# Bilinear interaction of 496 feature pairs: all of w in the first line of loads, one part turned in its own buffer, and the last batch tile stored in six groups, one of them by GpSimd's queue

## The chip, the cores and the metric

The kernel runs on one core of a Trainium2 chip. A core has five engines: TensorE (PE, matrix products), VectorE (DVE), ScalarE (ACT), GpSimd (POOL) and SyncE (SP, which here only issues transfers). Data moves between HBM and the on-chip memory SBUF through 16 DMA engines, which all queues share. The metric is the device time of one execution in microseconds (us), lower is better.

## The reference

There are 4096 samples with 32 feature vectors of 64 floats each, and for every pair of features (i, j) with i < j, 496 pairs in all, a 64 x 64 matrix. Each output vector is feature i times the pair's matrix, multiplied element by element with feature j. All is float32. The output has 4096 x 496 x 64 x 4 bytes = 520 MB; x has 33.6 MB, w 8.1 MB.

```python
B, F, D = (4096, 32, 64)
idx_i, idx_j = np.triu_indices(F, k=1)
vi = inputs[:, idx_i, :]
vj = inputs[:, idx_j, :]
vidots = jnp.einsum('bpd,pde->bpe', vi, W)
return vidots * vj
```

## The kernel before

The batch is cut into 16 blocks of 256 samples, each of two batch tiles of 128 samples (one to a partition). The 496 pairs are cut into five groups of 90, 97, 99, 105 and 105 pairs. The products of one tile and group gather in one of three buffers `ot`, and one store writes them out, 128 rows of up to 26.9 KB. A store must have landed before its buffer is filled again, which is three stores later.

```python
    bounds = [0, p0[3], p0[6] + CH, p0[11], p0[17], NP]      # 0, 90, 187, 286, 391, 496
    groups = list(zip(bounds[:-1], bounds[1:]))
    aside = (1, 3, 5, 7, 9, 11, 13)
    # ... (cut)
    xpool = ctx.enter_context(tc.tile_pool(name="xpool", bufs=2))
    tpool = ctx.enter_context(tc.tile_pool(name="tpool", bufs=4))
    opool = ctx.enter_context(tc.tile_pool(name="opool", bufs=3))
    psum = ctx.enter_context(tc.tile_pool(name="psum", bufs=4, space=bass.MemoryType.PSUM))
```

w comes in four parts (`wrows`) of 128, 128, 128 and 112 pairs, pairs in the partitions. Each part is ordered (`order_w`, four copies of a quarter each) and turned by TensorE (`turn_w`, four quarters) so that the summed index lies in the partitions. Ordered quarters lie in the four buffers `tmp`, which ACT's copies use too. The third and fourth part share one raw buffer, so the fourth is loaded when the third has been ordered.

```python
    def load_w(c: int, eng=nc.sync):
        a, b = wrows[c]
        pool, tag = ((opool, "ot"), (opool, "ot"), (const, "w3"), (const, "w3"))[c]
        raw[c] = pool.tile([P, D * D], F32, tag=tag, name=f"raw_{c}")
        eng.dma_start(out=raw[c][: b - a, :], in_=wflat[a:b])
```

[...] Every third block of x is loaded through it, 120 rows on 15 engines and the other 8 rows in two halves; `turn_engines` are transfers of a few bytes[...].

```python
    SWR = 120
    def load_fifteen(blk: int):
        rows = rows_of(x, blk).rearrange("(p k) f d -> p k f d", k=NB)
        dst = xs[blk]
        def part(ps: slice, fs: slice):
            tc.keep_in_program_order(nc.gpsimd.dma_start(out=dst[ps, :, fs, :], in_=rows[ps, :, fs, :]))
        part(slice(0, SWR), slice(0, F))
        turn_engines(1)
        for h in range(2):
            part(slice(SWR, P), slice(h * F // 2, (h + 1) * F // 2))
```

The first three batch tiles (`LEAD`) go through each group together, so that parts of w are needed one after another; 138 of the 1472 steps belong to them. Before the first step the loads are issued in one line, and `due` says ahead of which step a quarter of w is ordered and turned:

```python
    for c, orders, turns in (
        (1, (2, 4, 8, 10), (4, 7, 12, 15)),
        (2, (17, 22, 27, 32), (19, 24, 29, 34)),
        (3, (54, 54, 55, 55), (57, 60, 63, 66)),
    ):
        # ... (cut)
    no_aside = range(52, 67)
    # ... (cut)
    new_x(0)
    load_x(0, nc.sync, 0, 1)
    load_w(0)
    load_w(1)
    load_x(0, nc.sync, 1, NB)
    load_w(2)
    new_x(1)
    load_x(1, nc.sync)
    turn_engines(5)
```

A step computes up to 16 pairs: TensorE writes feature i times w to PSUM, then VectorE multiplies by feature j into `ot`. For some steps ScalarE copies PSUM aside to `tmp` and GpSimd multiplies.

```python
        if i in aside and c0 == 0 and s not in no_aside:
            tmp = tpool.tile([P, CH, 2, E2], F32, tag="tmp", name=f"tmp_{s}")
            nc.scalar.copy(tmp, src)
            nc.gpsimd.tensor_mul(dst, tmp, xj)
        else:
            nc.vector.tensor_mul(dst, src, xj)
        # ... (cut: at the group's end)
            nc.sync.dma_start(
                out=rows_of(out, blk).rearrange("(p k) n d -> p k n d", k=NB)[:, kt, n0 : pa + m, :],
                in_=ot[:, n0 - base : pa + m - base, :],
            )
    turn_engines(11)
```

Of the kernel before, what the change touches and what calls it, by code (L numbers as in the profile page):

```python
# [8 lines left out]
F32 = mybir.dt.float32  # L9
# [3 lines left out]
def kernel(  # L13
# [16 lines left out]
    nc = tc.nc  # L30

    B, F, D = x.shape
    P = 128
    NB = 2
    assert 2 * D == P and B % (NB * P) == 0
    NBLK = B // (NB * P)
    NP = F * (F - 1) // 2
    E2 = D // 2
    BANK = 512
    CH = BANK // E2  # L40
    RUN = 8
    p0 = [i * (F - 1) - i * (i - 1) // 2 for i in range(F)]


    bounds = [0, p0[3], p0[6] + CH, p0[11], p0[17], NP]
    groups = list(zip(bounds[:-1], bounds[1:]))
    cap = max(b - a for a, b in groups)

    aside = (1, 3, 5, 7, 9, 11, 13)

    cuts = [*range(0, NP, P), NP]
    wrows = list(zip(cuts[:-1], cuts[1:]))

    const = ctx.enter_context(tc.tile_pool(name="const", bufs=1))
    xpool = ctx.enter_context(tc.tile_pool(name="xpool", bufs=2))
    xtpool = ctx.enter_context(tc.tile_pool(name="xtpool", bufs=4))
    tpool = ctx.enter_context(tc.tile_pool(name="tpool", bufs=4))
    opool = ctx.enter_context(tc.tile_pool(name="opool", bufs=3))
# [7 lines left out]
    def rows_of(dram: bass.AP, blk: int) -> bass.AP:  # L66
        return dram[blk * NB * P : (blk + 1) * NB * P]

    def new_x(blk: int):

        wide = xpool.tile([P, NB, F * D + 16], F32, tag="xs", name=f"xs_{blk}")
        xs[blk] = wide[:, :, : F * D].rearrange("p k (f d) -> p k f d", d=D)

    def load_x(blk: int, eng, k0: int = 0, k1: int = NB):
        src = rows_of(x, blk).rearrange("(p k) f d -> p k f d", k=NB)
        eng.dma_start(out=xs[blk][:, k0:k1], in_=src[:, k0:k1])
# [4 lines left out]
    SWR = 120  # L81
# [4 lines left out]
    def turn_engines(k: int):  # L86
        n = k if k > 1 else 17
        c = used[0] % 8
        used[0] += 1
        src = x[: NB * n].rearrange("(p k) f d -> p k f d", k=NB)  # L90
        tc.keep_in_program_order(
            nc.gpsimd.dma_start(out=scratch[:n, :, c : c + 1], in_=src[:, :, 0, 0:1])  # L92
# [11 lines that stand above are left out]
        for h in range(2):  # L104
            part(slice(SWR, P), slice(h * F // 2, (h + 1) * F // 2))


    wflat = w.rearrange("p d e -> p (d e)")
    raw, wT = {}, {}
    EU = 2 * BANK // P  # L110
    NU = E2 // EU

    def load_w(c: int, eng=nc.sync):

        a, b = wrows[c]
        pool, tag = ((opool, "ot"), (opool, "ot"), (const, "w3"), (const, "w3"))[c]
        raw[c] = pool.tile([P, D * D], F32, tag=tag, name=f"raw_{c}")
        eng.dma_start(out=raw[c][: b - a, :], in_=wflat[a:b])

    def order_w(c: int, k: int, copy):  # L120
        r = wrows[c][1] - wrows[c][0]
        rp = tpool.tile([P, EU, 2, D], F32, tag="tmp", name=f"rp_{c}_{k}")
        src = raw[c][:r, :].rearrange("p (d h e) -> p e h d", h=2, d=D)
        copy(rp[:r], src[:, k * EU : (k + 1) * EU])  # L124
        return rp

    def turn_w(c: int, k: int, rp, copy):
        r = wrows[c][1] - wrows[c][0]
        home, tag, n = (wrows[c][0], "w3", r) if c == 3 else (0, "w", wrows[3][0])
        if home not in wT:  # L130
            wT[home] = const.tile([P, n, E2], F32, tag=tag, name=f"wT_{home}")
        pt = psum.tile([P, EU, P], F32, tag="ps", name=f"ptw_{c}_{k}")
        for n in range(EU):
            nc.tensor.transpose(  # L134
                pt[:, n, :r], rp[:r, n].rearrange("p h d -> p (h d)"), ident[:r, :r]
            )
        o = wrows[c][0] - home
        copy(wT[home][:, o : o + r, k * EU : (k + 1) * EU], pt[:, :, :r].rearrange("p e r -> p r e"))  # L138

    def turn_x(blk: int, k: int, q: int, copy):  # L140


        pt = psum.tile([P, RUN // 2, P], F32, tag="ps", name=f"ptx_{blk}_{k}_{q}")
        for u in range(RUN // 2):
            f = q * RUN + 2 * u
            nc.tensor.transpose(  # L146
                pt[:, u, :], xs[blk][:, k, f : f + 2, :].rearrange("p f d -> p (f d)"), ident
            )
        xT = xtpool.tile([P, 2, RUN // 2, P], F32, tag="xT", name=f"xT_{blk}_{k}_{q}")
        copy(xT[:, 0], pt)  # L150
        copy(xT[D:, 1], pt[:D])  # L151
        copy(xT[:D, 1], pt[D:])  # L152
        return xT


    steps = [
        (g, i, c0, min(CH, F - 1 - i - c0))
        for i in range(F - 1)
        for c0 in range(0, F - 1 - i, CH)
        for g, (a, b) in enumerate(groups)  # L160
        if a <= p0[i] + c0 < b
    ]
    NS = len(steps)
    first = {}
    for s, (_, i, _, _) in enumerate(steps):
# [4 lines left out]
    LEAD = 3  # L170
    NT = NBLK * NB
# [12 lines left out]
            due.setdefault(max(0, at), []).append(("x", t // NB, t % NB, q))  # L184
    for c, orders, turns in (
# [3 lines left out]
    ):  # L189
        for k in range(NU):  # L190
            due.setdefault(orders[k], []).append(("order", c, k))
            due.setdefault(turns[k], []).append(("turn", c, k))
    no_aside = range(52, 67)
    LATE = 6
    loads = {place[blk * NB, LATE]: blk + 1 for blk in range(2, NBLK - 1)}
    loads[place[LEAD, LATE]] = 2
# [3 lines left out]
    load_w(0)  # L200
    load_w(1)
    load_x(0, nc.sync, 1, NB)
    load_w(2)
    new_x(1)
    load_x(1, nc.sync)
    turn_engines(5)

    v, p, a = nc.vector.tensor_copy, nc.gpsimd.tensor_copy, nc.scalar.copy
    xT, rps = {}, {}
# [7 lines left out]
    ots = {}  # L217
    for s, (t, st) in enumerate(sched):
        blk, kt = divmod(t, NB)
        g, i, c0, m = steps[st]  # L220
        if s in loads:
            new_x(loads[s])
            if loads[s] % 3 == 0:
                load_fifteen(loads[s])
            else:
                load_x(loads[s], nc.scalar)
        for what, *args in due.get(s, ()):
            if what == "x":
                xT[tuple(args)] = turn_x(*args, a)
            elif what == "turn":  # L230
                turn_w(*args, rps.pop(tuple(args)), a)
            else:
                c, k = args
                rps[c, k] = order_w(c, k, (v, v, p, v)[c] if k % 2 == 0 else (v, v, p, a)[c])
                if (c, k) == (2, NU - 1):
                    load_w(3, nc.scalar)

        base, end = groups[g]
        pa = p0[i] + c0
        if pa == base:  # L240
            ots[t] = opool.tile([P, cap, D], F32, tag="ot", name=f"ot_{t}_{g}")
        ot = ots[t]
        ps = psum.tile([P, 2, CH, E2], F32, tag="ps", name=f"ps_{s}")
        for lo, hi in ((0, wrows[3][0]), wrows[3]):
            home, lo, hi = lo, max(pa, lo), min(pa + m, hi)
            if lo < hi:
                for h in range(2):
                    nc.tensor.matmul(  # L248
                        ps[:, h, lo - pa : hi - pa, :],
                        xT[blk, kt, i // RUN][h * D : (h + 1) * D, (i + h) % 2, i % RUN // 2, :],  # L250
                        wT[home][h * D : (h + 1) * D, lo - home : hi - home, :],
                        start=True,
                        stop=True,
                    )
        o = pa - base
        j = i + 1 + c0
        dst = ot[:, o : o + m, :].rearrange("p m (h e) -> p m h e", h=2)
        src = ps[:, :, :m, :].rearrange("p h m e -> p m h e")
        xj = xs[blk][:, kt, j : j + m, :].rearrange("p m (h e) -> p m h e", h=2)
        if i in aside and c0 == 0 and s not in no_aside:  # L260
            tmp = tpool.tile([P, CH, 2, E2], F32, tag="tmp", name=f"tmp_{s}")
            nc.scalar.copy(tmp, src)  # L262
            nc.gpsimd.tensor_mul(dst, tmp, xj)  # L263
        else:
            nc.vector.tensor_mul(dst, src, xj)  # L265

        ends = (p0[2], end) if s < NS and (t, g) == (0, 0) else (end,)
        if pa + m in ends:
            n0 = p0[2] if len(ends) > 1 and pa + m == end else base
            nc.sync.dma_start(  # L270
                out=rows_of(out, blk).rearrange("(p k) n d -> p k n d", k=NB)[:, kt, n0 : pa + m, :],
                in_=ot[:, n0 - base : pa + m - base, :],
            )
    turn_engines(11)


# [25 lines left out]
```

## Time and profile before

The time is 1342.57 us, the median of three executions (1342.16 to 1344.26). The profiled execution spans 1341.7 us.

| what | value |
|---|---|
| TensorE matmul busy | 1137.5 us, 85% of the span |
| VectorE, ScalarE, GpSimd busy | 954.2, 467.7, 543.0 us |
| bytes moved by DMA | 562.86 MB, mean 420 GB/s |
| HBM read, written | 41.68 MB, 520.09 MB |
| a store of 3.36 MB, from issue to landing | 16.4 us (median; another store is always in flight ahead of it) |
| product of 128 x 1024 on VectorE, on GpSimd | about 1.1 us, 2.36 us |

The page of a profile gives first each engine's busy time, then the span in 40 slices of 33.5 us with a digit of busy tenths for each engine, the granted TensorE clock, the DMA share and the rate in GB/s. Then come the DMA queues, the chain of work that ended last, the costliest groups of instructions and the DMA issues. Other views of the same trace give windows of any length, a timeline of one engine, or who waited for whom. L124 or L265 is a line of the kernel: L124 orders w, L134 and L138 turn it, L146 and L150 to L152 turn x, L248 is the product on TensorE, L262 and L263 are ScalarE's copy and GpSimd's product, L265 is VectorE's product, L270 the store.

### The profile page before, as it was taken

What the parts mean: (1) busy time and instruction counts of PE and PEld (TensorE: products, weight loads), DVE (VectorE), ACT (ScalarE), POOL (GpSimd) and SP (SyncE); (2) the same over time, 40 slices, a digit from 0 to 9 for tenths busy, and PEclk for the clock granted to TensorE, in tenths of its full rate; (3) what the DMA queues carried; (4) which work ended last, traced back from release to release, by engine and by line L of the source; (5) the groups of instructions that cost most, each with busy time, mean ns of one, the idle gap of its engine ahead of it and who ended that gap; (6) DMA issues with size and microseconds to landing.
All of it is one profiled execution on the core that took longest, in us unless ns stands there. A gap on an engine that the chain in (4) does not pass through costs nothing.

```text
span 1341.7 us, 16676 instructions
## 1 busy us (share of the span) xinstructions
PE 1137.5 (85%) x6656; PEld 605.0 (45%) x6656; DVE 954.2 (71%) x1262; ACT 467.7 (35%) x623; POOL 543.0 (40%) x252
## 2 busy tenths in 40 slices
PE   5989888878798797998888988788897879988884
PEld 3545444444344444444444544344444435444442
DVE  4778777767677676776767777577775767777774
ACT  4443333333233342333333333333333323333331
POOL 1723343444334443343453434434334433444441
PEclk9989999989999898998999999899998999999997
DMA  9899999999999999999999999999999999999997
GB/s 383 347 428 419 418 425 427 431 422 430 422 432 431 420 430 421 431 424 432 424 415 430 421 432 426 417 430 408 425 429 429 427 421 428 418 416 431 429 432 320
DMA packets 28895, 562.86 MB, mean 420 GB/s; under 512 B 3537, under 2 KB 3537, under 8 KB 3825
## 3 DMA queue, kind: packets, MB, share of 16 engines
q1 hardware_dynamic: 24176, 530.59, 93.0%
q10 hardware_dynamic: 2576, 20.71, 3.8%
q0 software_dynamic: 2064, 10.50, 2.0%
q8 instruction: 52, 0.85, 0.2%
q14 instruction: 27, 0.21, 0.0%
HBM read 41.68 MB, written 520.09 MB: 419 GB/s over the span
## 4 chain that ended last, share of the span: by engine, by line
DMA 55%; PE 22%; DVE 14%; POOL 5%; issue 2%; ACT 1%; SPq 0%; DVEq 0%; POOLq 0%; ACTq 0%
DMA out_dram<-ot 53%; PE ps L248 20%; DVE ot L265 13%; POOL ot L263 4%; DMA xs<-in_r_inputs_dram 2%; PE ptx L146 2%; ACT tmp L262 1%; PE ptw L134 1%; DVE rp L124 0%; POOL rp L124 0%; ACT xT L150 0%; ACT xT L152 0%; ACT xT L151 0%; DVEq L265 0%; POOL xs L100 0%
## 5 line engine op out<-in xcount | busy, mean ns | idle before, releaser
L265 DVE TENSOR_TENSOR ot<-ps,xs 128x1024 f32<-128x1024 f32 (+15 forms) x1252 | 940.9, 807 | 357.1 <-DMA out_dram<-ot 214.9
L248 PE MATMUL ps<-wT,xT 64*128 64x512 f32 (+13 forms) x6016 | 1046.1, 488 | 167.9 <-DVE ot L265 163.3
L263 POOL TENSOR_TENSOR ot<-tmp,xs 128x1024 f32<-128x1024 f32 x220 | 519.4, 2362 | 770.7 <-ACT tmp L262 592.6
L248 PEld LDWEIGHTS ps<-wT,xT 64*128 64x128 f32 x6016 | 534.7, 195 | 620.3 <-DVE ot L265 372.8
L262 ACT COPY tmp<-ps 128x1024 f32<-128x1024 f32 x220 | 222.7, 1012 | 498.0 <-PE ps L248 462.5
L150 ACT COPY xT<-ptx 128x512 f32<-128x512 f32 x128 | 74.9, 585 | 322.8 <-PE ptx L146 322.8
L146 PE MATMUL ptx<-ident,xs 128*128 128x128 f32 x512 | 84.8, 289 | 13.8 <-DMA xs<-in_r_inputs_dram 8.8
L146 PEld LDWEIGHTS ptx<-ident,xs 128*128 128x128 f32 x512 | 54.2, 142 | 85.9 <-DVE ot L265 60.0
L152 ACT COPY xT<-ptx 64x512 f32<-64x512 f32 x128 | 74.5, 582 | 1.5
L151 ACT COPY xT<-ptx 64x512 f32<-64x512 f32 x128 | 73.9, 577 | 1.5
L134 PE MATMUL ptw<-ident,rp 128*128 128x128 f32 (+1 forms) x128 | 19.1, 304 | 4.8 <-DVE rp L124 4.8
L134 PEld LDWEIGHTS ptw<-ident,rp 128*128 128x128 f32 (+1 forms) x128 | 16.1, 160 | 12.5 <-issue 5.4
L138 ACT COPY wT<-ptw 128x1024 f32<-128x1024 f32 (+1 forms) x15 | 14.8, 984 | 20.0 <-PE ptw L134 16.1
L124 DVE COPY rp<-raw 128x1024 f32<-128x1024 f32 (+1 forms) x9 | 12.8, 1453 | 10.6 <-DMA raw<-in_L_rec_W_dram 10.6
L100 POOL DMA_DIRECT2D xs<-in_r_inputs_dram x15 | 9.5, 636 | 0.0
L124 POOL COPY rp<-raw 128x1024 f32<-128x1024 f32 x4 | 8.0, 1990 | 0.1
L124 ACT COPY rp<-raw 112x1024 f32<-112x1024 f32 (+1 forms) x3 | 5.8, 1949 | 4.6 <-POOL ot L263 2.7
L92 POOL DMA_DIRECT2D scratch<-in_r_inputs_dram x7 | 6.2, 888 | 0.3 <-issue 0.3
L138 DVE COPY wT<-ptw 128x1024 f32<-128x1024 f32 x1 | 1.2, 1224 | 2.5 <-PE ptw L134 2.5
L150 ACT ACT_TABLE_LOAD x1 | 1.3, 1283 | 0.7 <-PEq L289 0.7
masks.py:199 POOL TENSOR_SCALAR_AFFINE_SELECT ident<-ident 128x128 f32<-128x128 f32 x1 | 0.3, 292 | 0.1
masks.py:197 POOL MEMSET ident<- 128x128 f32 x1 | 0.2, 204 | 0.3 <-POOLq L289 0.3
(4 smaller groups left out, 0.4 us busy)
## 6 DMA issues: line engine op xcount, KB each, us to landing
out_dram<-ot SPq DMA_DIRECT2D x64, 3360.0 KB, 16.4
out_dram<-ot SPq DMA_DIRECT2D x32, 3168.0 KB, 15.9
out_dram<-ot SPq DMA_DIRECT2D x32, 3104.0 KB, 17.0
out_dram<-ot SPq DMA_DIRECT2D x31, 2880.0 KB, 16.9
xs<-in_r_inputs_dram ACTq DMA_DIRECT2D x9, 2048.0 KB, 25.4
xs<-in_r_inputs_dram POOLq DMA_DIRECT2D x5, 1920.0 KB, 25.0
raw<-in_L_rec_W_dram SPq DMA_DIRECT2D x3, 2048.0 KB, 13.8
xs<-in_r_inputs_dram SPq DMA_DIRECT2D x2, 1024.0 KB, 10.3
```

The lines of the kernel that those rows point to most:

```text
L100: tc.keep_in_program_order(nc.gpsimd.dma_start(out=dst[ps, :, fs, :], in_=rows[ps, :, fs, :]))
L124: copy(rp[:r], src[:, k * EU : (k + 1) * EU])
L134: nc.tensor.transpose(pt[:, n, :r], rp[:r, n].rearrange("p h d -> p (h d)"), ident[:r, :r])
L138: copy(wT[home][:, o : o + r, k * EU : (k + 1) * EU], pt[:, :, :r].rearrange("p e r -> p r e"))
L146: nc.tensor.transpose(pt[:, u, :], xs[blk][:, k, f : f + 2, :].rearrange("p f d -> p (f d)"), ident)
L150: copy(xT[:, 0], pt)
L151: copy(xT[D:, 1], pt[:D])
L152: copy(xT[:D, 1], pt[D:])
L248: nc.tensor.matmul(ps[:, h, lo - pa : hi - pa, :], xT[blk, kt, i // RUN][h * D : (h + 1) * D, (i + h) % 2, i % RUN // 2, :], wT[home][h * ...
L262: nc.scalar.copy(tmp, src)
L263: nc.gpsimd.tensor_mul(dst, tmp, xj)
L265: nc.vector.tensor_mul(dst, src, xj)
```

## The change

It does three things. (a) The second block of x is loaded ahead of the third part of w, and the fourth part of w joins the first line of loads, instead of being loaded when the third has been ordered. For that the third part no longer has a raw buffer: it is loaded into the place where its turned form will stand, and all its quarters are ordered into `tmp` before the first one is turned back. As `tmp` is then full, ScalarE's copies of the first three tiles go into `ot` itself and GpSimd multiplies there. (b) The steps 52 to 66 use ScalarE and GpSimd too. (c) The last tile has six groups, of 90, 97, 99, 55, 100 and 55 pairs. The fifth goes out through GpSimd's queue, 120 rows (15 engines) and then 8 rows; its two halves lie one pair apart in `ot`, so that a row is two pieces. It is meant to fill the time in which no transfer runs near the start, and to shorten the last store and even out the DMA engines at the end.

```diff
+    last = [*bounds[:4], p0[13] + CH, p0[21], NP]
+    last_groups = list(zip(last[:-1], last[1:]))
+    HALVED = 4
+    half = p0[17] - last[HALVED]
 ...
+    def store_fifteen(dram: bass.AP, ot: bass.AP):
+        dst = dram.rearrange("p (c n) d -> p c n d", c=2)
+        src = ot[:, : 2 * half + 2, :].rearrange("p (c n) d -> p c n d", c=2)[:, :, :half, :]
+        for rows in (slice(0, SWR), slice(SWR, P)):
+            tc.keep_in_program_order(nc.gpsimd.dma_start(out=dst[rows], in_=src[rows]))
 ...
+    def load_w(c: int):
         a, b = wrows[c]
+        if c == 2:
+            raw[c] = home_of(c).rearrange("p r e -> p (r e)")
+        else:
+            pool, tag = (const, "w3") if c == 3 else (opool, "ot")
+            raw[c] = pool.tile([P, D * D], F32, tag=tag, name=f"raw_{c}")
+        nc.sync.dma_start(out=raw[c][: b - a, :], in_=wflat[a:b])
 ...
         (1, (2, 4, 8, 10), (4, 7, 12, 15)),
-        (2, (17, 22, 27, 32), (19, 24, 29, 34)),
-        (3, (54, 54, 55, 55), (57, 60, 63, 66)),
+        (2, (16, 18, 25, 27), (30, 33, 36, 39)),
+        (3, (46, 48, 50, 52), (56, 59, 62, 65)),
 ...
-    no_aside = range(52, 67)
 ...
     load_x(0, nc.sync, 1, NB)
-    load_w(2)
     new_x(1)
     load_x(1, nc.sync)
+    load_w(2)
+    load_w(3)
     turn_engines(5)
 ...
-                rps[c, k] = order_w(c, k, (v, v, p, v)[c] if k % 2 == 0 else (v, v, p, a)[c])
-                if (c, k) == (2, NU - 1):
-                    load_w(3, nc.scalar)
+                rps[c, k] = order_w(c, k, ((v, v, p, v), (v, v, p, a))[k % 2][c])
 ...
-        if i in aside and c0 == 0 and s not in no_aside:
-            tmp = tpool.tile([P, CH, 2, E2], F32, tag="tmp", name=f"tmp_{s}")
+        if i in aside and c0 == 0:
+            tmp = dst
+            if t >= LEAD:
+                tmp = tpool.tile([P, CH, 2, E2], F32, tag="tmp", name=f"tmp_{s}")
             nc.scalar.copy(tmp, src)
             nc.gpsimd.tensor_mul(dst, tmp, xj)
 ...
-            nc.sync.dma_start(
-                out=rows_of(out, blk).rearrange("(p k) n d -> p k n d", k=NB)[:, kt, n0 : pa + m, :],
-                in_=ot[:, n0 - base : pa + m - base, :],
-            )
-    turn_engines(11)
+            dram = rows_of(out, blk).rearrange("(p k) n d -> p k n d", k=NB)[:, kt, n0 : pa + m, :]
+            if halved:
+                store_fifteen(dram, ot)
+                turn_engines(4)
+            else:
+                nc.sync.dma_start(out=dram, in_=ot[:, n0 - base : pa + m - base, :])
```

More of the change, by code (lines that the diff above doesn't have):

```diff
@@ L46 @@
     groups = list(zip(bounds[:-1], bounds[1:]))
+    last = [*bounds[:4], p0[13] + CH, p0[21], NP]
+    last_groups = list(zip(last[:-1], last[1:]))
+    HALVED = 4
+    half = p0[17] - last[HALVED]
+    assert last[HALVED + 1] == p0[17] + half
     cap = max(b - a for a, b in groups)
+    assert 2 * half + 1 < cap
     aside = (1, 3, 5, 7, 9, 11, 13)
@@ L111, with home_of @@
     NU = E2 // EU
-    def load_w(c: int, eng=nc.sync):
-        a, b = wrows[c]
-        pool, tag = ((opool, "ot"), (opool, "ot"), (const, "w3"), (const, "w3"))[c]
-        raw[c] = pool.tile([P, D * D], F32, tag=tag, name=f"raw_{c}")
-        eng.dma_start(out=raw[c][: b - a, :], in_=wflat[a:b])
+    def home_of(c: int):
+        home, tag, n = (wrows[3][0], "w3", NP - wrows[3][0]) if c == 3 else (0, "w", wrows[3][0])
+        if home not in wT:
+            wT[home] = const.tile([P, n, E2], F32, tag=tag, name=f"wT_{home}")
+        return wT[home][:, wrows[c][0] - home : wrows[c][1] - home, :]
+    def load_w(c: int):
+        a, b = wrows[c]
+        if c == 2:
[4 more added lines that the diff above has]
+        nc.sync.dma_start(out=raw[c][: b - a, :], in_=wflat[a:b])
     def order_w(c: int, k: int, copy):
@@ L123, in order_w @@
         src = raw[c][:r, :].rearrange("p (d h e) -> p e h d", h=2, d=D)
-        copy(rp[:r], src[:, k * EU : (k + 1) * EU])
+        ins = copy(rp[:r], src[:, k * EU : (k + 1) * EU])
+        if c > 0:
+            tc.keep_in_program_order(ins)
         return rp
@@ L128, in turn_w @@
         r = wrows[c][1] - wrows[c][0]
-        home, tag, n = (wrows[c][0], "w3", r) if c == 3 else (0, "w", wrows[3][0])
-        if home not in wT:
-            wT[home] = const.tile([P, n, E2], F32, tag=tag, name=f"wT_{home}")
         pt = psum.tile([P, EU, P], F32, tag="ps", name=f"ptw_{c}_{k}")
@@ L136, in turn_w @@
             )
-        o = wrows[c][0] - home
-        copy(wT[home][:, o : o + r, k * EU : (k + 1) * EU], pt[:, :, :r].rearrange("p e r -> p r e"))
+        copy(home_of(c)[:, :, k * EU : (k + 1) * EU], pt[:, :, :r].rearrange("p e r -> p r e"))
     def turn_x(blk: int, k: int, q: int, copy):
@@ L153, in turn_x, with steps_of @@
         return xT
[L156 to L162, printed above, removed]
+    def steps_of(groups):
+        return [
+            (g, i, c0, min(CH, F - 1 - i - c0))
+            for i in range(F - 1)
+            for c0 in range(0, F - 1 - i, CH)
+            for g, (a, b) in enumerate(groups)
+            if a <= p0[i] + c0 < b
+        ]
+    steps, last_steps = steps_of(groups), steps_of(last_groups)
     NS = len(steps)
@@ L219 @@
         blk, kt = divmod(t, NB)
-        g, i, c0, m = steps[st]
+        g, i, c0, m = (last_steps if t == NT - 1 else steps)[st]
         if s in loads:
@@ L233 @@
                 c, k = args
-                rps[c, k] = order_w(c, k, (v, v, p, v)[c] if k % 2 == 0 else (v, v, p, a)[c])
-                if (c, k) == (2, NU - 1):
-                    load_w(3, nc.scalar)
-        base, end = groups[g]
+                rps[c, k] = order_w(c, k, ((v, v, p, v), (v, v, p, a))[k % 2][c])
+        base, end = (last_groups if t == NT - 1 else groups)[g]
+        halved = (t, g) == (NT - 1, HALVED)
         pa = p0[i] + c0
@@ L254 @@
                     )
-        o = pa - base
+        o = pa - base + (halved and pa - base >= half)
         j = i + 1 + c0
```

## The prediction

> **What bounds the kernel now.** I read the page from slice to stage: first the 40 slices (part 2), then windows of the first 114 us and the last 42 us, then the timelines of the engines beside the gaps, and last the landings that the trace records for each engine of a store.
>
> ```profile
> PE   5989888878798797998888988788897879988884
> DMA  9899999999999999999999999999999999999997
> GB/s 383 347 428 419 418 425 427 431 422 430 422 432 431 420 430 421 431 424 432 424 415 430 421 432 426 417 430 408 425 429 429 427 421 428 418 416 431 429 432 320
> ...
> q8 instruction: 52, 0.85, 0.2%
> ```
>
> The row to see is DMA: it is full in 38 of 40 slices, at some 427 GB/s, while PE, DVE, ACT and POOL are all under 90%. The kernel moves 562.86 MB, and at 427 GB/s that is 1318 us. The other 24 us are at the two ends, in slices 1, 2 and 40. Windows place them (columns: stretch, its length, busy us and count of PE, PEld, DVE, ACT and POOL, granted clock, DMA share, GB/s):
>
> ```profile
> core 0: us, PE busy (x) PEld busy (x) DVE busy (x) ACT busy (x) POOL busy (x), PEclk, DMA share, GB/s
> ...
> 26.00:28.00 2.00, 0.13 (x1) 0.16 (x2) 2.00 (x3) 0.00 (x0) 0.00 (x0) 1.00 0.46 193
> 28.00:34.00 6.00, 6.00 (x26) 3.27 (x27) 3.15 (x4) 2.76 (x4) 0.00 (x0) 0.72 1.01 422
> 34.00:40.00 6.00, 6.00 (x34) 2.80 (x30) 5.93 (x7) 2.02 (x2) 4.33 (x2) 1.00 0.32 133
> 40.00:60.00 20.00, 20.00 (x117) 11.24 (x116) 14.34 (x15) 10.13 (x10) 16.78 (x8) 1.00 0.99 420
> 60.00:66.00 6.00, 6.00 (x35) 2.97 (x35) 4.14 (x5) 3.77 (x5) 3.65 (x3) 1.00 1.04 316
> ...
> 1324.00:1326.00 2.00, 0.00 (x0) 0.00 (x0) 0.38 (x3) 0.00 (x0) 0.00 (x0) 0.88 0.78 336
> 1326.00:1333.00 7.00, 0.00 (x0) 0.00 (x0) 0.00 (x0) 0.00 (x0) 0.00 (x0) 0.50 1.00 430
> 1333.00:1342.00 9.00, 0.00 (x0) 0.00 (x0) 0.00 (x0) 0.00 (x0) 0.00 (x0) 0.50 0.08 34
> ```
>
> Three losses can be read here. Start: between 26 and 28 us DMA idles 2 x 0.54 = 1.1 us, between 34 and 40 us 6 x 0.68 = 4.1 us, because the first line of loads is done (the last lands at 27.7) and the second store isn't ready. From 60 to 66 us, while the fourth part of w is loaded, DMA is full but moves 316 GB/s instead of 427: 6 x 111 / 427 = 1.6 us. End: after 1333 us the DMA share is 0.08, about one engine of 16.
>
> Who makes the gap at the start, and what sets the last stores, stands in the timelines of PE and DVE (start, length, engine, line, then in brackets the idle time before and its releaser) and in the chain of work:
>
> ```profile
> 27.87 0.63 PE L146 MATMUL ptx<-ident,xs 128*128 128x128 f32 x4 [2.97 <-DMA xs<-in_r_inputs_dram]
> ```
> ```profile
> 1316.39 7.99 DVE L265 TENSOR_TENSOR ot<-ps,xs 128x896 f32<-128x896 f32 x14 [1.02 <-DMA out_dram<-ot]
> ```
> ```profile
> 1299.26 17.00 DMA out_dram<-ot
> 1316.26 0.03 issue
> 1316.29 0.05 DVEq L265
> 1316.34 0.04 issue
> 1316.39 7.86 DVE ot L265 x13
> 1324.25 0.13 DVEq L298
> ```
>
> PE stands 2.97 us for the second block of x, which is last in the line of loads. At the end, the last group's DVE work can't start before 1316.3, when the store three places earlier has left its buffer, and its own store goes out at 1324.4. The landings of that last store, engine by engine, say what the page doesn't: 14 of its engines are done between 1333.6 and 1334.5, the fifteenth at 1336.7, the sixteenth at 1340.0. One engine is 6.3 us behind the middle. The store of 1299.26 shows the same: eight engines by 1309.9, the last at 1316.3.
>
> [...] 52 packets of 0.85 MB / 52 = 16.4 KB, 0.93 us each, one about every 26 us. The lag of the slowest engine grows from store to store by 0.25 to 0.3 us per 7.9 us, and 0.93 x 7.9 / 26 = 0.28: all these fetches sit on one engine. [...] around the load on 15 engines at 1191 us the lag falls from 6.2 to 3.2 us. [...] Here the granted clock is 0.72 from 28 to 34 us, just after the idle time of 2.97 us.
>
> **The change at the start.** The second block of x moves ahead of the third part of w, and the fourth part of w joins the first line. Loads run at 427 GB/s, so 2.1 MB is 4.9 us: x block 1 lands at 27.7 - 4.9 = 22.8, w part 2 at 27.7, w part 3 (1.84 MB, 4.3 us at that rate, 5.8 at the rate of 316) at 32 to 33.5. PE's 2.97 us go, so the work of tiles 1 and 2 comes 2.8 us earlier: the stores now issued at 38.5, 45.4, 52.6, 60.8, 67.8 and 72.8 go out at about 35.7, 42.6, 49.8, 58, 65 and 70. The first two stores (2.95 MB, 6.9 us) wait behind the loads and fill DMA to 39 or 40, and the next three keep it full: 46.5 against the 42.6 above, 53.5 against 49.8, 60.5 against 58. So the gaps of 1.1 and 4.1 us close, and slow loading no longer holds stores: of 1.6 us I count half, 0.8.
>
> Must compute follow that pace later? At 76 us DVE now waits 3.5 us for a buffer, since the load of w part 3 is in the way; with DMA some 6 us ahead, that buffer (the store issued at 60.8, landing at 76.1) is free by 69, before it is wanted at 70. PE is busy 34.4 of 38 us from 76 to 114, so it is the pace there: the store now issued at 104.45 can come at 104.45 - 2.8 - 3.5 = 98, where DMA, always full, would reach it at 97. That is just enough. Turning w part 2 in place forces all four copies (POOL, 1.99 us each, unchanged in number) before the first write back; their steps move from 17-32 to 16-27, so POOL's sum stays. ACT's and POOL's share of the products in the steps 52 to 66 takes four DVE products of about 1.1 us off DVE and adds 2.36 us each to POOL, which is free then. Start in sum: 1.1 + 4.1 + 0.8 = 6.0 us.
>
> **The change at the end.** The last tile's groups of 90, 97, 99, 105, 105 pairs become 90, 97, 99, 55, 100, 55. The group of 100 (3.28 MB, 25.6 KB a row) goes out by GpSimd: 8 rows each on 15 engines, then one row each on eight[...]. The late engine writes 1 row instead of 8 and is spared 7 x 25.6 = 179 KB; at 427 / 16 = 26.7 GB/s that is 6.7 us, so it would end at about 1340.0 - 6.7 = 1333.3. It is no longer last, but the others aren't then done.
>
> Their path, in times of the kernel before: the first 55 pairs are ready when POOL's product ends, 1314.2, and their store follows the one that eight engines finish at 1317.4; 1.80 MB take 4.2 us, so these engines are free at 1321.6. The 100 pairs need the buffer that comes free at 1316.3, and then 4 products in 3.9 us and 4 in 3.1 us: issue at 1323.5, and with 0.7 us of GpSimd's issue and about 1 us to the first byte, bytes from 1325.2. So DMA stands 3.6 us for want of data, but for the late engines. 8 rows are 205 KB, 7.7 us, to 1332.9, and a ninth row 1 us more, 1333.9; the last 55 pairs (ready at 1328.5, in time) take 4.2 us: 1337.1 to 1338.1. Gain against 1340.0: 2 to 3 us; I take 2.6.
>
> **Sum.** 1342.6 - 6.0 - 2.6 = 1334.0 us.
>
> **Rivals.** (1) Compute becomes the bound from 60 to 114 us, since the stores' lead over DMA is only 2 to 3 us there. For it: PE is full from 28 to 74 us, and POOL has 16.8 busy of 20 us in 40 to 60. Against it: the clock of 0.72 may not occur again, which returns up to 6 x 0.28 = 1.7 us. Then the start brings 3 us and the time is 1337. (2) The late engine isn't the one left out, or GpSimd's store spreads over all 16: the end keeps 1340.0 and adds the gap of 3.6 us, and only the start is left: 1337 to 1340. The drop from 6.2 to 3.2 us at the load on 15 engines speaks against it. (3) The gap before the store of 100 pairs doesn't occur, because DMA still holds work then: the end brings up to 5 us and the time is 1331.5. (4) Without idle stretches at the start the late engine catches up less, later buffers come late, and part of the 6 us is given back by 1324; the first relief load at about 190 us, when the lag is only 1.9 us, should absorb that.
>
> **Range and chances.** The start can bring 3 to 8, the end -1 to 5: 1329 to 1340 should hold it 8 times in 10. All of slices 1, 2 and 40 hold some 24 us, and 2% is 27, so over 2% faster is hardly possible: 0.01. Over 2% slower would need a new stall of 27 us, as if the load into w's own buffer held up its first readers: 0.01. Within 2%: 0.98.
>
> **What would show it.** DMA share over 0.95 from 4 to 60 us and no wait of PE for x over 1 us; the store now issued at 104.4 at about 98; no DVE wait at 76. At the end the share falls from full in about 1321 minus 6, comes back 3 to 4 us later, and falls within 2 us at the end instead of 7. If DMA idles between 40 and 110, rival 1 holds; if one engine still lands over 4 us after the rest, rival 2.

## The result, and the profile after

The changed kernel takes 1351.91 us (median of six executions, 1350.82 to 1352.86) against 1343.04 us for the kernel before in the same session: a ratio of 1.0067 with a 95% interval of 1.0054 to 1.008. It is 9 us slower; the prediction was 8.6 us faster. The loss lies at one end. First the page, the DMA rows of the 40 slices:

```profile
DMA  9999999999999999999999999999999999999995
GB/s 366 431 424 424 424 421 430 425 426 430 424 432 418 426 430 423 431 423 428 418 418 431 420 431 420 425 420 411 432 419 433 425 422 417 412 429 433 426 425 160
```

Slice 2 rises from 347 to 431 GB/s: the gap at the start is closed. Slice 40 falls from 320 to 160. The windows at the start, to be held against those of before:

```profile
core 0: us, PE busy (x) PEld busy (x) DVE busy (x) ACT busy (x) POOL busy (x), PEclk, DMA share, GB/s
...
26.00:28.00 2.00, 2.00 (x13) 1.03 (x12) 2.00 (x3) 1.24 (x3) 0.00 (x0) 1.00 1.07 360
28.00:35.00 7.00, 7.00 (x40) 3.56 (x38) 6.64 (x6) 3.51 (x4) 2.36 (x1) 1.00 0.97 282
35.00:40.00 5.00, 3.75 (x22) 1.96 (x22) 4.37 (x5) 1.63 (x3) 0.51 (x1) 1.00 0.99 420
40.00:60.00 20.00, 19.22 (x110) 10.30 (x106) 15.48 (x16) 8.02 (x10) 20.00 (x10) 1.00 1.02 436
60.00:66.00 6.00, 6.00 (x39) 3.45 (x38) 3.38 (x5) 4.79 (x6) 3.51 (x2) 1.00 1.01 435
```

The DMA engines have no idle stretch any more, PE doesn't wait for x, and its clock stays at 1.00. One thing in it isn't good: from 28 to 35 us, while the fourth part of w is loaded, full DMA engines move only 282 GB/s. Now the end of the same kernel:

```profile
1312.00:1316.00 4.00, 2.96 (x10) 1.75 (x12) 2.39 (x4) 0.00 (x0) 0.00 (x0) 0.50 0.93 398
1316.00:1320.00 4.00, 4.00 (x18) 2.12 (x18) 2.64 (x3) 0.83 (x2) 0.00 (x0) 0.64 0.41 174
1320.00:1324.00 4.00, 3.82 (x30) 2.04 (x26) 3.93 (x5) 0.92 (x2) 0.94 (x2) 1.00 0.06 25
1324.00:1328.00 4.00, 2.45 (x22) 1.50 (x20) 3.07 (x9) 0.00 (x0) 1.00 (x2) 1.00 0.96 205
1328.00:1332.00 4.00, 0.00 (x0) 0.00 (x0) 0.00 (x0) 0.00 (x0) 0.00 (x0) 0.64 1.01 199
1332.00:1336.00 4.00, 0.00 (x0) 0.00 (x0) 0.00 (x0) 0.00 (x0) 0.00 (x0) 0.50 1.02 270
1336.00:1340.00 4.00, 0.00 (x0) 0.00 (x0) 0.00 (x0) 0.00 (x0) 0.00 (x0) 0.50 0.88 266
1340.00:1344.00 4.00, 0.00 (x0) 0.00 (x0) 0.00 (x0) 0.00 (x0) 0.00 (x0) 0.50 0.68 241
1344.00:1348.00 4.00, 0.00 (x0) 0.00 (x0) 0.00 (x0) 0.00 (x0) 0.00 (x0) 0.50 0.25 88
```

The two columns at the right are to be read together. Up to 1324 us the share falls to 0.06: the predicted gap before the fifth store. From 1324 to 1332 the share is full, 0.96 and 1.01, but the rate is about 202 GB/s, half of the usual 427. The engines are busy, but each packet takes twice as long. The trace's records of packets say the same: the pieces of 12.8 KB of the fifth store take 953 ns on average from 1324 to 1328 us, while a row of 14.1 KB of the store ahead of it takes 529 ns, the rate at which 12.8 KB would take 480. The timelines show when GpSimd issues the fifth store's two transfers, and that DVE waits for a buffer before it can fill that store:

```profile
1323.06 1.35 POOL L118 DMA_DIRECT2D out_dram<-ot  x2 [12.51 <-DVE ot L291]
```
```profile
1312.69 1.55 DVE L291 TENSOR_TENSOR ot<-ps,xs 128x128 f32<-128x128 f32 x3 [5.69 <-DMA out_dram<-ot]
```

GpSimd issues both transfers by 1324.4, and the first packets start at 1324.4. Up to 1325.2 15 pieces are in flight, and of the 16 landings of the 120 rows one comes at 1325.3 and the other 15 from 1337.2 to 1346.3, as if one engine had none of these rows. The last store of SP goes out at 1327.1, in time, and then waits its turn among the slow pieces: its last landing is at 1349.1.

### The profile page after: what moved, and what is told of

It reads as the page before. It is cut to its first block, busy times and chain, and to the rows that moved or that the text cites. A ratio compares the mean times of both kernels' runs of the same rounds, so it can differ in the third digit from the quotient of the medians.

```text
span 1351.1 us, 16693 instructions
## 1 busy us (share of the span) xinstructions
PE 1137.5 (84%) x6656; PEld 601.6 (45%) x6656; DVE 950.8 (70%) x1258; ACT 471.4 (35%) x627; POOL 553.7 (41%) x258
## 4 chain that ended last, share of the span: by engine, by line
DMA 58%; PE 19%; DVE 14%; POOL 4%; issue 2%; ACT 1%; DVEq 0%; SPq 0%; POOLq 0%; ACTq 0%
DMA out_dram<-ot 57%; PE ps L271 17%; DVE ot L291 13%; POOL ot L289 4%; PE ptx L167 1%; DMA raw<-in_L_rec_W_dram 1%; PE ptw L156 1%; ACT tmp L288 1%; POOL rp L147 0%; DVE rp L147 0%; DVEq L291 0%; POOL xs L107 0%; ACT wT L159 0%; POOL scratch L99 0%; SPq L301 0%
## 5 line engine op out<-in xcount | busy, mean ns | idle before, releaser
L289 POOL TENSOR_TENSOR ot<-tmp,xs 128x1024 f32<-128x1024 f32 x203 | 478.8, 2359 | 706.0 <-ACT tmp L288 516.3
L288 ACT COPY tmp<-ps 128x1024 f32<-128x1024 f32 x203 | 205.5, 1012 | 473.5 <-PE ps L271 437.5
L289 POOL TENSOR_TENSOR ot<-ot,xs 128x1024 f32<-128x1024 f32 x21 | 49.8, 2377 | 51.9 <-ACT ot L288 51.8
L288 ACT COPY ot<-ps 128x1024 f32<-128x1024 f32 x21 | 21.3, 1013 | 25.5 <-PE ps L271 14.5
L147 POOL COPY rp<-wT 128x1024 f32<-128x1024 f32 x4 | 7.8, 1964 | 0.0
L118 POOL DMA_DIRECT2D out_dram<-ot x2 | 1.4, 678 | 12.5 <-DVE ot L291 12.5
## 6 DMA issues: line engine op xcount, KB each, us to landing
out_dram<-ot SPq DMA_DIRECT2D x62, 3360.0 KB, 16.4
xs<-in_r_inputs_dram ACTq DMA_DIRECT2D x9, 2048.0 KB, 25.3
```

The costliest lines, as they stand in the source:

```text
L147: ins = copy(rp[:r], src[:, k * EU : (k + 1) * EU])
```

## The experiments

The question was first whether the end alone costs the time, and then which of its properties: the cut into six groups, GpSimd's queue, the half rows with a gap between them, or the 120 rows.

**e1_start.** The changed start, the end of the kernel before.

```diff
-    last = [*bounds[:4], p0[13] + CH, p0[21], NP]
+    last = bounds
-    HALVED = 4
+    HALVED = -1
...
+    turn_engines(11)
```

> The changed start with the end of the kernel before (five groups, all stores by SP). If the loss lies in the end alone, the start keeps the 3.7 us that the stores of the last tile were ahead by: 1339.3 us, 1338 to 1341. If the changed start also costs something that its trace hides, 1343 or more.

Measured: 1338.83 us, ratio 0.997 (0.9958 to 0.9981). The start is good and brings 4.0 us against the 1342.87 of the kernel before in that session; the end costs 1351.91 - 1338.83 = 13.1 us (the kernel before differs by 0.2 us between the two sessions).

**e2_sp_six.** Six groups, all stores by SP.

```diff
-    HALVED = 4
+    HALVED = -1
...
+    turn_engines(11)
```

> Six groups, but the fifth store goes by SP's queue as one row of 25.6 KB a partition. If the six groups are harmless: the late engine goes on from 1324.5 with 205 and 113 KB at 26.7 KB/us to 1336.4, 1339.5 us in all (1338 to 1341). If cutting the last tile itself costs the time (the gap before the fifth store), 1345 or more.

Measured: 1337.65 us, ratio 0.9961 (0.9946 to 0.9976).

```profile
1316.00:1320.00 4.00, 4.00 (x22) 1.79 (x20) 3.34 (x4) 1.75 (x3) 0.00 (x0) 0.87 0.31 131
1320.00:1324.00 4.00, 3.70 (x28) 1.91 (x26) 4.00 (x7) 0.00 (x0) 0.00 (x0) 1.00 0.55 233
1324.00:1328.00 4.00, 1.30 (x14) 0.90 (x12) 1.80 (x7) 0.00 (x0) 0.00 (x0) 0.91 0.96 410
1328.00:1332.00 4.00, 0.00 (x0) 0.00 (x0) 0.00 (x0) 0.00 (x0) 0.00 (x0) 0.50 1.01 430
1332.00:1336.00 4.00, 0.00 (x0) 0.00 (x0) 0.00 (x0) 0.00 (x0) 0.00 (x0) 0.50 0.54 227
```

The same gap stands between 1316 and 1323 us, and no cost of it shows in the time: the late engine, which lands its part of the fourth store at 1323.1, works through it, and afterwards all are together. The 16 landings of the last store lie between 1334.5 and 1335.3; in the kernel before they were spread over 6.4 us. So the gap evens the engines out without any relief.

**e3_gp128.** The fifth store through GpSimd's queue in the same two pieces, but 128 rows in one transfer. Theory A in the expectations is that the 120 rows are what makes the store slow.

```diff
-        for rows in (slice(0, SWR), slice(SWR, P)):
+        for rows in (slice(0, P),):
...
-                turn_engines(4)
+                turn_engines(11)
```

> The fifth store through GpSimd's queue, with the same two pieces of 12.8 KB a row, but as one transfer of all 128 rows on 16 engines. Theory A [...]: the pieces take about 480 ns, as in other stores, and the time is 1340 (1338 to 1342). Rival B (stores by GpSimd's queue are slow): pieces of about 950 ns and 1350 to 1353. Rival C (pieces of half a row with a gap are slow): the same as B.

Measured: 1338.79 us, 0.9969 (0.9956 to 0.9982).

```profile
1324.00:1328.00 4.00, 1.00 (x12) 0.63 (x10) 1.46 (x6) 0.00 (x0) 0.00 (x0) 0.93 0.98 410
1328.00:1332.00 4.00, 0.00 (x0) 0.00 (x0) 0.00 (x0) 0.00 (x0) 0.00 (x0) 0.50 1.00 425
```

Full share and full rate; the pieces take 491 ns. GpSimd's queue and the half rows are cleared.

**e4_sp120.** 120 and 8 rows, both through SP's queue.

```diff
-            tc.keep_in_program_order(nc.gpsimd.dma_start(out=dst[rows], in_=src[rows]))
+            nc.sync.dma_start(out=dst[rows], in_=src[rows])
...
-                turn_engines(4)
+                turn_engines(11)
```

> The fifth store as 120 and 8 rows in the same pieces, but both through SP's queue. Theory A: the pieces still take about 950 ns on 15 engines and the time is 1348 to 1354. Rival B: pieces of about 480 ns and 1338 to 1342. Rival C: slow, as A says; e3 tells A from C.

Measured: 1351.1 us, 1.0061 (1.0046 to 1.0076), as slow as the change itself.

```profile
1320.00:1324.00 4.00, 3.29 (x28) 1.85 (x26) 4.00 (x10) 0.00 (x0) 0.00 (x0) 1.00 0.91 212
1324.00:1328.00 4.00, 0.00 (x0) 0.00 (x0) 0.00 (x0) 0.00 (x0) 0.00 (x0) 0.66 1.00 209
```

The half rate comes along with the 120 rows into the other queue: the pieces take 915 ns until the sixth store joins in at 1325.4. So rival B is out a second time; C fell with e3.

Why 120 rows halve the rate (953 ns a piece in the changed kernel against 480, a factor of 2.0) is not shown by these runs, and the trace names neither the row nor the engine of a packet. That it depends on which rows move together was the author's assumption; the next pair tries it.

**e5_far_rows and e6_near_rows.** In both, GpSimd issues the fifth store as 16 transfers of 8 rows. Only the choice of the rows differs. The expectations put rows 4 apart at the usual 480 ns a piece and neighbours at a quarter of the rate; that factor was the author's assumption.

```diff
-        for rows in (slice(0, SWR), slice(SWR, P)):
-            tc.keep_in_program_order(nc.gpsimd.dma_start(out=dst[rows], in_=src[rows]))
+        for j in range(4):                            # e5: rows 4 apart
+            for b in (0, 64, 32, 96):
+                rows = slice(b + j, b + j + 29, 4)
+                tc.keep_in_program_order(nc.gpsimd.dma_start(out=dst[rows], in_=src[rows]))
+        for n in range(16):                           # e6 instead: neighbours
+            rows = slice(8 * n, 8 * n + 8)
+            tc.keep_in_program_order(nc.gpsimd.dma_start(out=dst[rows], in_=src[rows]))
...
-                turn_engines(4)
+                turn_engines(11)
```

> The fifth store through GpSimd's queue as 16 transfers of 8 rows[...]. The 8 rows of a transfer are 4 apart (0, 4, .. 28, then 64, 68, .. 92, and so on)[...] pieces of about 480 ns; only the 16 issues of 0.6 us on GpSimd slow it: 1338 to 1343 us. If few rows in a transfer are what is slow, pieces well over 480 ns and 1350 or more.

> The same 16 transfers of 8 rows, but 8 neighbouring rows each[...] about a quarter of the rate, 3.28 MB at some 108 GB/s is 30 us after 1324.5, pieces of 1500 to 2000 ns, 1355 to 1363 us.[...]

Measured: 1342.69 us with rows 4 apart, 0.9998 (0.9989 to 1.0007), and 1354.02 us with neighbours, 1.0082 (1.0063 to 1.01). Windows of the first, then of the second:

```profile
1320.00:1324.00 4.00, 3.28 (x28) 1.83 (x26) 3.98 (x10) 0.00 (x0) 4.00 (x8) 1.00 0.57 225
1324.00:1328.00 4.00, 0.00 (x0) 0.00 (x0) 0.00 (x0) 0.00 (x0) 3.70 (x7) 0.69 0.98 328
1328.00:1332.00 4.00, 0.00 (x0) 0.00 (x0) 0.00 (x0) 0.00 (x0) 1.11 (x2) 0.50 1.08 374
```
```profile
1320.00:1324.00 4.00, 3.70 (x30) 1.91 (x26) 4.00 (x7) 0.12 (x1) 1.77 (x4) 1.00 0.39 56
1324.00:1328.00 4.00, 1.75 (x16) 1.19 (x16) 2.25 (x7) 0.00 (x0) 2.67 (x5) 1.00 0.85 128
```

From 1320 to 1324 us, before the sixth store joins in, the rows 4 apart move 225 GB/s at a share of 0.57 and the neighbours 56 at 0.39: a busy engine moves 2.7 times as much with rows 4 apart. The mean time of all pieces that start before the first row of the sixth store:

```
kernel          rows of a transfer      pieces   a piece of 12.8 KB   against 480 ns
e3_gp128        128                       226          491 ns             1.0
e5_far_rows     8 rows, 4 apart            99          512 ns             1.1
after           120, then 8                68          946 ns             2.0
e4_sp120        120, then 8                84          915 ns             1.9
e6_near_rows    8 neighbours               56         1448 ns             3.0
```

In e6 only the first 11 pieces, up to 1324 us, come to the factor that was expected, 1936 ns or 4.0; later ones take anything from 479 to over 2500 ns, and from 1328 us on 910 on average. Why they differ isn't shown. e6 was expected at 1355 to 1363 us and came out a little better.

So neither GpSimd's queue (491 ns in e3) nor few rows in a transfer (512 ns in e5) make a store slow, but which rows a transfer holds does: 512 ns with 8 rows 4 apart, 1448 with 8 neighbours. What causes it isn't shown. The choice of the rows sets which partitions of SBUF are read together, but also which rows of the output in HBM, 254 KB apart from one partition to the next, are written at the same time. No run of a store separates the two. In e8 below the slow load reads rows that lie one after another in HBM, which speaks for the partitions.

**e7_early.** The store of 120 and 8 rows is kept but stands one group earlier, as the fourth of six, with whole stores of SP beside and after it; for that all six groups are cut anew.

```diff
-    last = [*bounds[:4], p0[13] + CH, p0[21], NP]
+    last = [0, p0[2] + CH, p0[5], p0[7] + CH, p0[12], p0[18], NP]
-    HALVED = 4
-    half = p0[17] - last[HALVED]
-    assert last[HALVED + 1] == p0[17] + half
+    HALVED = 3
+    half = p0[9] + CH - last[HALVED]
+    assert last[HALVED + 1] == p0[9] + CH + half
```

> The store on 15 engines is kept but comes earlier: the last tile has groups of 77, 68, 67, 94, 99 and 91 pairs and the fourth goes by GpSimd, so that two whole stores of SP run beside and after it. Theory A: [...] the late engine is relieved: 1332 to 1338 us, and the 16 engines land within 3 us of each other. If a store of 120 rows costs its double time wherever it stands, 1343 or more.

Measured: 1350.99 us, 1.0062 (1.0047 to 1.0077). This was a miss: other traffic doesn't hide the loss.

```profile
1312.00:1316.00 4.00, 4.00 (x27) 2.13 (x26) 4.00 (x6) 1.37 (x3) 3.48 (x3) 1.00 0.90 193
1316.00:1320.00 4.00, 3.76 (x28) 1.98 (x26) 4.00 (x6) 0.38 (x1) 0.00 (x0) 1.00 0.96 196
1320.00:1324.00 4.00, 2.29 (x20) 1.48 (x20) 2.84 (x8) 0.00 (x0) 0.00 (x0) 0.92 1.23 318
1324.00:1328.00 4.00, 0.00 (x0) 0.00 (x0) 0.00 (x0) 0.00 (x0) 0.00 (x0) 0.50 0.89 300
```

Its pieces of 12.0 KB take 832 ns from 1317 to 1324 us. Of the 18 rows of 25.3 KB that SP starts beside them in this stretch, ten take the usual 940 to 947 ns and eight take 1196 to 3438: some of the other traffic is slowed too.

**e8_w3_128.** The fourth part of w has 112 rows. Here it is loaded as 128 rows, of which 16 are loaded twice and not used. The end is that of e1.

```diff
     def load_w(c: int):
         a, b = wrows[c]
+        if c == 3:
+            a = b - P
...
-        r = wrows[c][1] - wrows[c][0]      # in order_w and turn_w
+        r = P
+        z = P - (wrows[c][1] - wrows[c][0])
...
-        copy(home_of(c)[:, :, ...], pt[:, :, :r]...)
+        copy(home_of(c)[:, :, ...], pt[:, :, z:r]...)
```

> The changed start with the end of the kernel before, and the fourth part of w loaded as 128 rows (16 of them a second time, not used) instead of 112. [...] the 112 rows[...] are why that load runs at 270 GB/s; 128 rows take 4.9 us instead of 6.7, so the DMA engines are 1.8 us ahead, and the time is 1337 us (1336 to 1338.5) against 1338.8 with 112 rows. If 112 rows aren't the cause, the extra 0.26 MB cost 0.6 us: 1339.4.

Measured: 1338.53 us, 0.9965 (0.9953 to 0.9978), not to be told from e1. The load itself did what was expected. The line of its window, before it that of e1:

```profile
28.00:35.00 7.00, 7.00 (x42) 3.87 (x40) 6.63 (x6) 3.51 (x5) 2.36 (x1) 1.00 1.00 313
28.00:35.00 7.00, 7.00 (x40) 3.64 (x38) 6.64 (x6) 3.51 (x4) 2.36 (x1) 1.00 1.02 395
```

The rate is 395 GB/s instead of 313, or 282 in the changed kernel, and the 2.1 MB have landed on the middle engine at 32.9 us, where the 1.84 MB of 112 rows land at 34.1 (e1) and 34.6 (the changed kernel). So the number of rows is what slows that load. What this is worth in the end can't be read. The store issued at 104.45 us in the kernel before comes 6.1 us earlier in e8's profile and 4.3 in e1's, but in the profiles of the other kernels with 112 rows anything from 4.5 to 6.6. The same experiment with six groups, **e10_six_w128**, leaves it as open:

> Six groups with all stores by SP, and the fourth part of w loaded as 128 rows. The first line ends about 1 us sooner; if that isn't lost again to the pace of the middle, 1336.7 us against 1337.7; else the same within 0.5 us.

Measured: 1338.55 us, 0.9964 (0.9952 to 0.9977); no gain over e2, and in its profile that store comes only 3.9 us earlier.

**e9_relief_2, e11_relief_all, e12_relief_none.** The fifth store was meant to relieve a late engine. What is relief worth in the loads of x, and do these take double the time, as the store did? All three have the end of e2; only the blocks that are loaded as 120 and 8 rows differ.

```diff
-            if loads[s] % 3 == 0:            # 5 blocks
+            if loads[s] % 2 == 1:            # e9: 7 blocks
+            if loads[s] > 2:                 # e11: 13 blocks
+            if loads[s] > 99:                # e12: none
```

> Six groups with all stores by SP, and every second block of x loaded on 15 engines (7 loads) instead of every third (5). If the late engine, through the buffers it frees late, sets the pace of the middle: each load on 15 engines takes about 4.5 us off its lag, which grows by some 2.7 us a block, so the pace improves and the time is 1328 to 1334 us against 1337.7. [...] (a double time for 2 MB is 4.6 us each): 1340 to 1348. If neither matters: 1337 to 1338.

> As e9_relief_2, with all blocks from the fourth on (13 loads) on 15 engines. Late engine sets the pace: 1325 to 1332 us, the lag near zero at the end. [...] 13 - 5 = 8 more at up to 4.6 us, 1345 to 1375.

> As e2_sp_six, with no load on 15 engines. Late engine sets the pace: its 52 fetches of 0.93 us, 48 us in all, then fall on the end and on the buffers; 5 reliefs of 4.5 us are gone and the time is 1345 to 1360 us. If the reliefs cost what they bring: 1336 to 1339.

Measured: 1335.23 us with 7 loads, 0.9946 (0.9927 to 0.9964); 1338.14 with 13, 0.9965 (0.9956 to 0.9974); 1350.14 with none, 1.0054 (1.0039 to 1.0069). The mean lag of a store's last engine behind its middle, from 200 to 1300 us, falls with the number of loads: 6.65, 4.89 (e2), 4.28 and 3.40 us. So the first five reliefs are worth 1350.14 - 1337.65 = 12.5 us, 2.5 us each, and all 13 no more than the five. The loss without relief builds up in the middle: the first store of the last tile goes out at 1286.7 us in e2 and at 1298.0 in e12, so 11.3 of the 12.5 us are there before the end begins. In e12 those blocks also come through ACT's queue instead of GpSimd's, and no run separates this from the cut into 120 and 8 rows. The expected 1325 to 1332 for all blocks was a miss: the lag is nearly halved against none, and yet the time is no better than with five. Why isn't settled. The pieces of these loads are not slowed: all but a few of 3120 take 309 ns, as in the loads of ACT.

e9_relief_2 has the lowest median of all that ran, ahead of both kernels, a little above the 1328 to 1334 that were expected. It was expected to gain on e2 (1337.65), but its executions run from 1332.77 to 1338.61, and the 2.4 us between the two can't be told from noise.

## Why the prediction was wrong

**The bound and the late engine: right.** DMA is full from 4 us to the end of the third store of the last tile, and the late engine is real: without the five loads that relieve it, the kernel loses 12.5 us.

**The start: right in kind, too large.** It was put at 1.1 + 4.1 + 0.8 = 6.0 us; e1 gives 4.0. Both gaps close. The third term has the wrong sign: the slow load of the fourth part of w doesn't become harmless when it is alone. At 282 GB/s for 7 us it loses 7 x 145 / 427 = 2.4 us in the changed kernel's profile, and at 313 in e1's 1.9, against 1.6 before, which is -0.3 to -0.8 instead of +0.8. That would leave 4.4 to 4.9, and the interval of e1's ratio, 2.6 to 5.6 us, holds this. The first rival shows in e1's profile and not in the changed kernel's. The window from 90 to 102 us, e1 first:

```profile
90.00:102.00 12.00, 12.00 (x88) 7.01 (x88) 9.24 (x13) 6.82 (x10) 8.70 (x4) 1.00 0.91 386
90.00:102.00 12.00, 12.00 (x90) 6.78 (x88) 8.47 (x15) 7.86 (x11) 8.29 (x4) 1.00 0.99 421
```

PE is full in both, and DMA is at 0.91 in one and at 0.99 in the other. The store issued at 104.45 us in the kernel before came 4.3 us earlier in the first and 5.6 us in the second, against the 6.3 that were worked out.

**The end: this is the step that failed.** The sum had "8 rows are 205 KB, 7.7 us, to 1332.9". The gap before it came as described, but lasted from 1317.9 to 1324.4: the fourth store went out at 1310.6, as worked out and moved by the start's 3.7 us, the fifth at 1323.1 instead of 1319.8, because PE's granted clock was 0.50 from 1312 to 1316 us and 0.64 to 1320, and DVE waited for it (0.34 to 0.92 us before each of four products). e2 has such a delay too (its fifth store goes out at 1321.5) and is still 5.2 us faster than the kernel before. The 8 rows, though, which were to take 7.7 us, landed 13 to 22 us after the first byte, on the last engine at 1346.3. The sixth store, queued among their pieces, landed at 1349.1, where the prediction's own path, moved by the start, ends at 1334. The term took the rate of 128 rows, 427 / 16 GB/s an engine, for 120 rows, which got half of it: some 202 GB/s in all from 1324 to 1332 us, 953 ns a piece instead of 480. The trace of before held a hint that was read wrongly: DMA engines at a share of 1.04 that moved 316 GB/s from 60 to 66 us, during a load of 112 rows. It was taken as a matter of loading beside stores.

**The rivals.** None of the four allowed for a slower transfer. The second came nearest by name, but its reason, that GpSimd's store would use all 16 engines, is the opposite: with the DMA share at 0.98 and 1.00, in e3, it is harmless. That the engine left out is the late one, and that it then gets one of the 8 rows, was an assumption and can't be read, as the trace names no engine. The third, an end without a gap, didn't occur. In e2 the gap costs nothing, because the late engine would have set the end and works on through it; so the 3.6 us that the prediction held against the six groups were not there, and with all last landings within 0.8 us a relief had nothing left to win.

## What to carry to other kernels

When the DMA share is full and the rate is not, look at the number of rows: here a store of 120 rows ran at half the rate of 128 rows, through either queue (946 and 915 ns a piece against 491), and a load of 112 rows at two thirds to three quarters (282 and 313 GB/s against 427). So measure the pieces of a transfer of fewer rows by themselves, and with another choice of rows, before a kernel relies on it. A lag of one engine at the end may need no relief at all: groups cut small enough that the other engines wait let it catch up (in e2 the last landings lie within 0.8 us, against 6.4 before).

## What the runs showed of the hardware that was not expected

- A store's rate depends on which rows its transfers hold: pieces of 12.8 KB took 491 ns with 128 rows in one transfer, 946 with 120 and then 8, and with 8 neighbours to a transfer 1936 at first and 1448 on average. Sixteen small transfers whose rows lie 4 apart ran at 512 ns a piece, so nearly the full rate doesn't need one transfer of 128 rows; the price is 16 issues of 0.55 us on GpSimd.
- Loads of 120 rows in the middle of the kernel show no such loss (309 ns for 8 KB, as with 128 rows), while a store of 120 rows between stores does (e7), and so does a load of 112 rows beside hardly anything else (984 ns for 16 KB from 28 to 34 us in the changed kernel, against 612 for the parts of 128 rows). Why the first are spared isn't shown.
- One DMA engine becomes late, by 6.65 us behind the middle on average without relief, and stores wait for it: five loads of 120 and 8 rows were worth 12.5 us of 1350. That the 52 packets of 16.4 KB of the queue that the page calls "instruction" make it late is the prediction's inference from the growth of the lag (0.25 to 0.3 us a store; 0.28 worked out from 0.93 us a packet and one in about 26 us); the trace doesn't name a packet's engine.
